# Four graph-attention layers in one kernel: nodes in strided chunks, attention vectors spread by TensorE, another order of the opening, a last step that ends chunk by chunk

## The chip, the core and the metric

The kernel runs on one NeuronCore of a Trainium2 chip, in one launch. The metric is device time in microseconds (us), from the first to the last instruction of the core. Before the change the time is 2699.22 us (median of 3 runs, 2696.39 to 2703.35).

The engines are named as in the profile: PE is TensorE's matmul, PEld its loading of the stationary operand, DVE is VectorE, ACT is ScalarE, POOL is GpSimd. SP only issues transfers. A "q" behind a name (SPq, ACTq) stands for the engine's own sequencer, where a DMA is issued. Each engine works through its instructions in the order in which the program gives them, so an instruction that waits holds up all that stand behind it on that engine.

## The reference

Sixteen graphs of 1024 nodes with 256 features go through four attention layers, all over the same adjacency matrix. Cut to what matters (`heads` is 4 with 64 features each in layers 0 and 2, and 1 with 256 features in layers 1 and 3):

```python
# x: (16, 1024, 256) float32, adj: (1024, 1024) int32 (about 3% ones)
for W, a in layers:
    h = maximum(layernorm(x), 0)
    q = (h @ W).reshape(B, N, heads, D)
    e = leaky_relu(q . a_src [:, i]  +  q . a_dst [:, j])    # for every pair i, j of nodes
    e = where(adj, e, -inf)
    x = x + act(softmax(e, axis=j) @ q)    # act: elu in layers 0 to 2, relu in layer 3
```

The 1024 x 1024 matrix of attention weights is made anew for each graph, layer and head: 16 x (4 + 1 + 4 + 1) = 160 times.

## The kernel before

A graph and a layer together are a **step**; there are 64 of them, numbered in the order in which the kernel takes them (four graphs, the streams, are in work at a time; the first six steps belong to the streams 0, 1, 2, 0, 3, 2). A step has a *preparation*, the *weights*, the *aggregation* and a *finish*. While one step is aggregated, the preparation of the next but one or so is put between the groups of its matmuls, by an agenda: the number of each piece says behind which group it comes.

Nodes lie on 128 partitions in 8 chunks. Before the change, node `c * 128 + p` is on partition `p` in chunk `c`, so that a graph's 1 MB comes in as pieces of 1 KB:

```python
def load(b, parts=1):
    xs[b] = xpool.tile([P, C, F], F32, name="x")          # P = 128, C = 8, F = 256
    xb = x[b].rearrange("(c p) f -> p c f", p=P)
    for i in range(parts):
        q = slice(i * C // parts, (i + 1) * C // parts)
        nc.sync.dma_start(out=xs[b][:, q], in_=xb[:, q])
```

The attention vectors of a layer are put on all partitions by the DMA itself, and two dot products with each row of W give the columns that are appended to W (on DVE):

```python
def vectors(queue=nc.sync):
    st["a"] = prep.tile([P, HALF, H, D], F32, name="e")
    for part in range(2):
        queue.dma_start(out=st["a"][:, part],
            in_=bass.AP(tensor=avs[l].tensor, offset=avs[l].offset + part * D,
                        ap=[[0, P], [hs, H], [1, D]]))      # step 0: the same row, 128 times
def columns():          # 4 products and 4 sums on DVE, and the squares for bound()
    ...
def bound():            # a matmul with ones, then DVE and POOL: biases for the exponentials
    ...
```

The adjacency is read once, in 8 blocks of 128 rows. For each block DVE takes the sign as bf16, PE turns it, DVE makes the 0/1 mask of layers 0 and 1 and ACT that of layers 2 and 3:

```python
def fetch_rows():  nc.sync.dma_start(out=st["raw"], in_=adj[c * P:(c + 1) * P, :])
def sign():        nc.vector.tensor_scalar(st["sgn"][:, 0], st["raw"], -1.0, 1.0, op0=max, op1=min)
def turn():        # 8 transposes of 128 x 128; four PSUM buffers hold the results
    for jc in range(C):
        nc.tensor.transpose(pm[:, jc, :], st["sgn"][:, 0, jc * P:(jc + 1) * P], identb)
def positive():    nc.vector.tensor_scalar(masks[0][:, :, c * P:(c + 1) * P], st["pm"], 0.0, None, is_gt)
def nonzero():     nc.scalar.activation(masks[1][:, :, c * P:(c + 1) * P], st["pm"], AF.Square)
```

The preparation of a step is a list of 20 pieces: `stats(0)`, `stats(1)` (DVE: `bn_stats` of four chunks each, then the reciprocal deviations), `normalise(0)`, `normalise(1)` (ACT), for each half two `transpose` (PE, evacuated by ACT with a relu) and four `project` (PE: four matmul instructions per chunk of nodes; ACT and POOL evacuate), then `factors` (ACT: exponentials), `rows` (PE turns the row factors, ACT copies them, SP writes them to DRAM), `fetch_heads` (SP reads them back, spread over all partitions: `gs`), and an empty one.

The weights of a head are 8 tiles of 128 x 1024, made from the spread row factors `g` (copied to PSUM by ACT), the column factors and the mask:

```python
def weights(n, h, jc):                                     # 18 buffers
    w = work.tile([P, N], F32, name="w", bufs=WBUFS)
    nc.vector.scalar_tensor_tensor(w, st["g", h], st["rcol"][:, jc, h:h + 1], mask[:, jc, :],
                                   op0=ALU.max, op1=ALU.mult)

def aggregate(n, h, i0, per):      # a group: four chunks of a head, or one where heads = 1
    ...                            # PE: sums over jc of w.T @ [q, 1]
    nc.scalar.activation(st["y"][:, i0:i0 + per, h, :], acc, AF.Copy)
```

`finish` works on all 8 chunks of the step: DVE takes the reciprocals, POOL scales in two halves, DVE adds to x in two halves, SP stores in two halves:

```python
def divide():      nc.vector.reciprocal(st["r"], st["y"][:, :, :, D])
def scaled(half):  nc.gpsimd.tensor_tensor(yh, yh, r..., op=mult)
def add(half):     nc.vector.scalar_tensor_tensor(xh, yh, 0.0, xh, op0=max, op1=add)   # last layer
def store(half):   nc.sync.dma_start(out=out[b, half * HALF * P:...].rearrange("(c p) f -> p c f", p=P), in_=...)
```

The opening, up to the main loop:

```python
load(0, 2)                                   # x of graph 0 in two halves, SP
layer[0][0](nc.scalar)                       # vectors of layer 0, on ACT's queue
load_weights(0, nc.scalar)                   # W of layer 0, on ACT's queue
for c in range(C): blocks[c][0]()            # adjacency, SP
load(1); load_weights(1)
...
first[0](); first[1](); first[2]()           # step 0: stats, stats, normalise
layer[0][1]()                                # columns
first[3](); ...                              # normalise; sign, turn, bound, transpose, project
...                                          # and the masks, in turns
for _ in range(2): agenda.pop(0)[2]()        # stats of step 1
emit_tiles(C, must=True)                     # weights of step 0, head 0
prepare(-1)                                  # the rest of the preparation of step 1
for i in range(2, STREAMS):
    load_weights(i); load(i)                 # x of graphs 2 and 3
# main loop: groups of step 0, ...
```

The agenda of step 1 is `[-2] * 10 + [-1] * 10`: all of its preparation stands ahead of the first group of step 0. The pieces `vectors`, `columns` and `bound` of the layers 1, 2 and 3 come behind the groups 0, 1 and 7 counted from step 0 group 1, step 3 group 3 and step 5 group 3.

Of the kernel before, what the change touches and what calls it, by code (L numbers as in the profile page):

```python
# [20 lines left out]
F32 = mybir.dt.float32  # L24
# [18 lines left out]
AFTER_FOUR = (-3, -2, -1, 0, 1, 1, 2, 2, 3, 3, 4, 4, 5, 5, 6, 6, 7, 8, 8, 10)  # L43
SOON = (0, 0, 1, 2, 3, 3, 4, 4, 5, 5, 5, 5, 6, 6, 7, 7, 8, 9, 9, 11)
AFTER_ONE = (0, 1, 2, 3, 4, 4, 5, 5, 6, 6, 7, 7, 8, 8, 9, 9, 10, 11, 11, 13)
LATE = (0, 0, 1, 1, 2, 2, 3, 3, 3, 3, 3, 3, 4, 4, 4, 4, 5, 6, 6, 8)


# [9 lines left out]
def kernel(ctx: ExitStack, tc: tile.TileContext, x, adj, ws, avs, out):  # L58
# [47 lines left out]
    def weight_columns(l):  # L106

        H, slope, hs, _ = LAYERS[l]
        D = F // H
        st = {}  # L110

        def vectors(queue=nc.sync):
            st["a"] = prep.tile([P, HALF, H, D], F32, name="e")
            for part in range(2):
                queue.dma_start(
                    out=st["a"][:, part],
                    in_=bass.AP(tensor=avs[l].tensor, offset=avs[l].offset + part * D,
                                ap=[[0, P], [hs, H], [1, D]]),
                )

        def columns():
            for k in range(K):
                for part in range(2):
                    prod = st["a"][:, 2 + part]
                    nc.vector.tensor_mul(
                        prod, wx[l][:, k, 0:F].rearrange("p (h d) -> p h d", h=H),
                        st["a"][:, part])
                    nc.vector.tensor_reduce(
                        wx[l][:, k, F + part * H:F + (part + 1) * H], prod, AX.X, ALU.add)
            st["sq"] = small.tile([P, K, H], F32, name="sq", bufs=1)  # L130
            wd = wx[l][:, :, F + H:F + 2 * H]
            nc.vector.tensor_tensor(st["sq"], wd, wd, op=ALU.mult)

        def bound():

            pn = ps_p.tile([P, H], F32, name="pp")
            for k in range(K):
                nc.tensor.matmul(pn, lhsT=ones, rhs=st["sq"][:, k, :], start=(k == 0),
                                 stop=(k == K - 1))
            top = small.tile([P, 1], F32, name="top", bufs=1)  # L140
            nc.vector.tensor_reduce(top, pn, AX.X, ALU.max)
            nc.gpsimd.tensor_tensor(top, top, half1, op=ALU.pow)
            nc.gpsimd.tensor_scalar(cbias[l], top, 16.01, None, op0=ALU.mult)
            nc.gpsimd.tensor_scalar(nbias[l], top, -16.01 * slope, None, op0=ALU.mult)
            nc.gpsimd.tensor_scalar(rbias[l], top, -16.01 * (1.0 - slope), SHIFT,
                                    op0=ALU.mult, op1=ALU.add)

        return vectors, columns, bound

    pairs = {}  # L150

    def mask_rows(c):

        st = {}

        def fetch_rows():
            st["raw"] = work.tile([P, N], I32, name="w", bufs=WBUFS)
            nc.sync.dma_start(out=st["raw"], in_=adj[c * P:(c + 1) * P, :])

        def sign():  # L160
            st["sgn"] = work.tile([P, 2, N], BF16, name="w", bufs=WBUFS)
            nc.vector.tensor_scalar(st["sgn"][:, 0], st["raw"], -1.0, 1.0, op0=ALU.max,
                                    op1=ALU.min)

        def turn():

            if c < HALF:
                if c % 2 == 0:
                    pairs[c // 2] = ps_g.tile([P, 2, C, P], BF16, name="g")
                pm = pairs[c // 2][:, c % 2]  # L170
            else:
                pm = ps_acc.tile([P, C, P], BF16, name="acc")
            st["pm"] = pm
            for jc in range(C):
                nc.tensor.transpose(pm[:, jc, :], st["sgn"][:, 0, jc * P:(jc + 1) * P], identb)

        def positive():
            nc.vector.tensor_scalar(masks[0][:, :, c * P:(c + 1) * P], st["pm"], 0.0, None,
                                    op0=ALU.is_gt)

        def nonzero():
            nc.scalar.activation(masks[1][:, :, c * P:(c + 1) * P], st["pm"], AF.Square)

        return fetch_rows, sign, turn, positive, nonzero

    def load(b, parts=1):
        xs[b] = xpool.tile([P, C, F], F32, name="x")
        xb = x[b].rearrange("(c p) f -> p c f", p=P)
        for i in range(parts):
            q = slice(i * C // parts, (i + 1) * C // parts)  # L190
            nc.sync.dma_start(out=xs[b][:, q], in_=xb[:, q])

    def preparation(n):
# [6 lines left out]
        def stats(half):  # L200
            if half == 0:
                st["bn"] = small.tile([P, C, 6], F32, name="bn")
            bn = st["bn"]
            for c in range(half * HALF, (half + 1) * HALF):
                nc.vector.bn_stats(bn[:, c, :], xs[b][:, c, :])  # L205
            if n == 0:
                combine(slice(half * HALF, (half + 1) * HALF), nc.vector)
            elif half == 1:
                combine(slice(0, C), nc.gpsimd)

        def combine(q, engine):

# [12 lines left out]
            engine.tensor_tensor(rstd, rstd, dev, op=ALU.add)  # L225
            nc.gpsimd.tensor_tensor(rstd, rstd, neghalf[:, q], op=ALU.pow)  # L226
            engine.tensor_tensor(shift, m0, m1, op=ALU.add)  # L227
            engine.tensor_tensor(shift, shift, rstd, op=ALU.mult)
            engine.tensor_scalar(shift, shift, -0.5, None, op0=ALU.mult)  # L229

# [84 lines left out]
    def aggregate(n, h, i0, per):  # L315
# [7 lines left out]
        for q in range(per):  # L323
            for jc in range(C):

                for o in range((i0 + q) * P, (i0 + q + 1) * P, cols):
                    nc.tensor.matmul(acc[o % P:o % P + cols, q, :],  # L327
                                     lhsT=st["w", h, jc][:, o:o + cols],
                                     rhs=st["whx"][:, jc, h, :], start=(jc == 0),
                                     stop=(jc == C - 1))  # L330
        nc.scalar.activation(st["y"][:, i0:i0 + per, h, :], acc, AF.Copy)  # L331

    def finish(n):
# [37 lines left out]

        def store(half):
            nc.sync.dma_start(
                out=out[b, half * HALF * P:(half + 1) * HALF * P, :].rearrange(
                    "(c p) f -> p c f", p=P), in_=xs[b][:, half * HALF:(half + 1) * HALF, :])
            if half == 1 and b + STREAMS < B:
                load(b + STREAMS)

# [61 lines left out]
    for n, (b, l) in enumerate(steps):  # L440
# [9 lines left out]
        if free > start + kind[0]:  # L450
            kind = LATE
            start = max(free, agenda_of[-1][0] + 5)
        agenda_of.append([start + k for k in kind] if n > 1 else [-2] * 10 + [-1] * 10)
        if n > 2:

            was = agenda_of[n - 1]
# [3 lines left out]
    with tc.manual_schedule():  # L460
        blocks = [mask_rows(c) for c in range(C)]
        layer = [weight_columns(l) for l in range(L)]
        load(0, 2)
        layer[0][0](nc.scalar)
        load_weights(0, nc.scalar)
        for c in range(C):
            blocks[c][0]()
        load(1)
        load_weights(1)
        nc.scalar.activation(warm, half1, AF.Exp)  # L470
        nc.vector.tensor_copy(identb, ident)
        first = [piece for _, piece in preparation(0)]

        turned, signed, masked = iter(range(C)), iter(range(C)), iter((0, 4, 5, 6, 1, 2, 3, 7))

        def sign_and_mask(second=True):
            c = next(signed, None)
            if c is not None:
                blocks[c][1]()
                blocks[c][2]()  # L480
            if second:
                c = next(turned, None)
                if c is not None:
                    blocks[c][3]()

        def other_mask(count):
            for _ in range(count):
                c = next(masked, None)
                if c is not None:
                    blocks[c][4]()  # L490

        first[0]()
        first[1]()
        first[2]()
        layer[0][1]()
        first[3]()
        sign_and_mask(False)
        layer[0][2]()
        sign_and_mask()
        for at in (4, 10):  # L500
            first[at]()
            first[at + 1]()
            sign_and_mask()
            first[at + 2]()
            first[at + 3]()
            sign_and_mask()
            other_mask(1)
            first[at + 4]()
            first[at + 5]()
            sign_and_mask()  # L510
            other_mask(1)
        for piece in first[16:]:
            piece()
        sign_and_mask()
        other_mask(C)
        done["prepared"] = 1
        plan(1)
        planned = 2
        for _ in range(2):
            agenda.pop(0)[2]()  # L520
        emit_tiles(C, must=True)
        prepare(-1)
        for i in range(2, STREAMS):
            load_weights(i)
            load(i)

        for l, at in ((1, 1), (2, 8 * 3 + 3), (3, 8 * 5 + 3)):
            for i, piece in zip((0, 1, 7), layer[l]):
                later[at + i] = piece
        for n in range(len(steps)):  # L530
            for k, (h, i0, per) in enumerate(groups(n)):
# [13 lines left out]
                emit_tiles(min(done["tiles"] + ahead, done["free"] + WBUFS))  # L545
            for _, piece in ending:
                piece()
            ending = finish(n)
        for _, piece in ending:
            piece()  # L550


def order_of_steps(B, L):
# [30 lines left out]
```

## Time and profile before

| | |
|---|---|
| span of the profiled execution | 2700.4 us |
| PE busy | 2567.4 us, 95% of the span |
| PEld busy | 2271.1 us, 84% |
| DVE busy | 1903.4 us, 70% |
| ACT busy | 1228.1 us, 45% |
| POOL busy | 987.8 us, 37% |
| DMA: mean rate, share of the main queue | 48 GB/s, 13.7% |
| mean granted clock of TensorE | 0.984 of full speed |
| transfers of x: 15 of 1024 KB, 2 of 512 KB | in pieces of 1 KB |

The page of the profile gives busy times and a strip of 40 slices. Where an engine that is busy nearly all the time stands still is seen better in tables of chosen stretches (busy time of each engine in each) and in the timeline. In the timeline a row has the start, the time taken from the first to the last instruction of the row, the engine, the line of the kernel, the operation, what it writes and reads with shapes, and how many instructions are merged in the row. The bracket at its end says how long the engine had been idle and what released it.

### The profile page before, as it was taken

The numbers are of one execution on the slowest core, as the hardware profiler recorded it, in microseconds if no ns is written. First come the engines' busy times: TensorE is split into PE (matmuls) and PEld (weight loads), VectorE is DVE, ScalarE is ACT, GpSimd is POOL, SyncE is SP. The second block draws the span as 40 slices with busy tenths as digits, with TensorE's granted clock in tenths as the row PEclk, the third lists the DMA queues.
The fourth block names the chain that finished last, engine by engine and source line by source line (L and its number), as shares of the span: only waits on it lengthen the run. The fifth ranks groups of instructions, "written<-read, shape, count | busy, mean of one in ns | idle before, by whom it ended". The sixth has DMA issues, their size and how long they took to land.

```text
span 2700.4 us, 89532 instructions
## 1 busy us (share of the span) xinstructions
PE 2567.4 (95%) x40080; PEld 2271.1 (84%) x40080; DVE 1903.4 (70%) x2059; ACT 1228.1 (45%) x3338; POOL 987.8 (37%) x1234
## 2 busy tenths in 40 slices
PE   4899999999999999999999999999999999999998
PEld 3787888888888888888888888888888888788876
DVE  5796586477785688667875778748687567678742
ACT  4343445445444544554444554544435444444431
POOL 2143433532514434344242353452342443443321
PEclk8899999999999999999999999999999999999999
DMA  4211101112012111002211201101202110111011
GB/s 137 76 42 37 30 26 41 35 62 81 26 61 67 42 42 33 18 33 72 73 34 49 72 33 43 41 25 57 80 27 72 63 41 19 34 40 43 33 33 55
DMA packets 63694, 130.12 MB, mean 48 GB/s; under 512 B 6224, under 2 KB 41808, under 8 KB 63312
## 3 DMA queue, kind: packets, MB, share of 16 engines
q1 hardware_dynamic: 61984, 123.88, 13.7%
q8 instruction: 316, 5.18, 0.8%
q10 hardware_dynamic: 1328, 0.52, 0.1%
q14 instruction: 66, 0.54, 0.1%
HBM read 106.95 MB, written 17.43 MB: 46 GB/s over the span
## 4 chain that ended last, share of the span: by engine, by line
PE 82%; DVE 8%; ACT 4%; issue 3%; POOL 2%; DMA 1%; DVEq 0%; SPq 0%; ACTq 0%; POOLq 0%
PE acc L327 61%; PE pp L255 17%; DVE w L311 6%; PE pp L243 4%; DVE bn L205 1%; ACT xn L235 1%; DMA wx<-in_L_gnn_W 1%; POOL rstd L226 1%; ACT whx L257 1%; ACT g L306 0%; ACT e L361 0%; ACT whx L261 0%; PE pp L282 0%; ACT y L331 0%; POOL y L352 0%
## 5 line engine op out<-in xcount | busy, mean ns | idle before, releaser
L327 PE MATMUL acc<-whx,w 128*64 128x65 f32 x36864 | 1951.8, 242 | 41.3 <-DVE w L311 30.4
L327 PEld LDWEIGHTS acc<-whx,w 128*64 128x64 f32 x36864 | 1768.0, 146 | 223.5 <-issue 69.9
L311 DVE SCALAR_TENSOR_TENSOR w<-g,rcol,mask 128x1024 f32<-128x1024 f32 x1280 | 1544.1, 1274 | 440.5 <-ACT g L306 394.6
L331 ACT ACTIVATE y<-acc 128x260 f32<-128x260 f32 (+1 forms) x512 | 196.5, 384 | 1089.8 <-PE acc L327 1089.7
L255 PE MATMUL pp<-wx,hT 128*128 128x258 f32 (+1 forms) x2048 | 514.1, 394 | 5.7 <-ACT hT L244 3.2
L352 POOL TENSOR_TENSOR y<-y,r 128x1024 f32<-128x1024 f32 x128 | 242.3, 1897 | 618.0 <-DVE r L348 614.4
L255 PEld LDWEIGHTS pp<-wx,hT 128*128 128x128 f32 x2048 | 376.2, 191 | 75.1 <-ACT whx L261 6.0
L266 POOL TENSOR_TENSOR whx<-whx 128x256 f32<-128x256 f32 x256 | 160.0, 629 | 461.5 <-ACT whx L264 460.4
L368 POOL TENSOR_TENSOR x<-x,e 128x1024 f32<-128x1024 f32 x96 | 226.6, 2365 | 274.7 <-DVE e L367 250.1
L235 ACT ACTIVATE xn<-x,shift,rstd 128x256 f32<-128x256 f32 x512 | 264.2, 590 | 135.0 <-POOL shift L229 122.4
L367 DVE SCALAR_TENSOR_TENSOR e<-e,y 128x1024 f32<-128x1024 f32 x96 | 117.7, 1226 | 197.1 <-ACT e L361 197.1
L257 ACT ACTIVATE whx<-pp,nbias 128x4 f32<-128x4 f32 (+1 forms) x512 | 134.9, 264 | 166.4 <-PE pp L255 155.2
L243 PE MATMUL pp<-ident,xn 128*128 128x128 f32 x1024 | 158.7, 288 | 43.7 <-ACT xn L235 34.1
L205 DVE BATCH_NORM_STATS2 bn<-x 128x6 f32<-128x256 f32 x512 | 173.0, 407 | 28.5 <-DMA x<-in_x 25.8
L243 PEld LDWEIGHTS pp<-ident,xn 128*128 128x128 f32 x1024 | 117.1, 144 | 82.5 <-ACT xn L235 43.8
L306 ACT ACTIVATE g<-gs 128x1024 f32<-128x1024 f32 x160 | 162.4, 1018 | 8.4 <-DVE w L311 5.4
L244 ACT ACTIVATE hT<-pp 128x512 f32<-128x512 f32 x256 | 142.9, 592 | 26.6 <-PE pp L243 24.5
L261 ACT ACTIVATE whx<-pp,whx 128x256 f32<-128x256 f32 x256 | 121.4, 474 | 0.0
L220 POOL TENSOR_TENSOR dev<-bn 128x8 f32<-128x8 f32 x63 | 16.1, 256 | 276.5 <-DVE bn L205 276.5
L361 ACT ACTIVATE e<-e 128x1024 f32<-128x1024 f32 x96 | 100.8, 1050 | 30.0 <-POOL e L357 30.0
L226 POOL TENSOR_TENSOR rstd<-rstd,neghalf 128x8 f32<-128x8 f32 (+1 forms) x65 | 107.0, 1646 | 19.2 <-DVE shift L227 14.3
L357 POOL TENSOR_SCALAR e<-y 128x1024 f32<-128x1024 f32 x96 | 99.8, 1040 | 8.4
(58 smaller groups left out, 550.7 us busy)
## 6 DMA issues: line engine op xcount, KB each, us to landing
gs<-grow SPq DMA_DIRECT2D x160, 512.0 KB
out<-x SPq DMA_DIRECT2D x32, 512.0 KB
x<-in_x SPq DMA_DIRECT2D x15, 1024.0 KB
w<-in_adj SPq DMA_DIRECT2D x8, 512.0 KB
x<-in_x SPq DMA_DIRECT2D x2, 512.0 KB
wx<-in_L_gnn_W SPq DMA_DIRECT2D x3, 256.0 KB
e<-in_L_gnn_a SPq DMA_DIRECT2D x6, 128.0 KB
grow<-gT SPq DMA_DIRECT2D x32, 16.0 KB
```

The lines of the kernel that those rows point to most:

```text
L205: nc.vector.bn_stats(bn[:, c, :], xs[b][:, c, :])
L235: nc.scalar.activation(xn[:, q, :], xs[b][:, c, :], AF.Identity, bias=st["shift"][:, c:c + 1], scale=st["rstd"][:, c:c + 1])
L243: nc.tensor.transpose(pt[:, q, :], st["xn", half][:, q, k * P:(k + 1) * P], ident)
L255: nc.tensor.matmul(pw, lhsT=st["hT", half][:, k, q * P:(q + 1) * P], rhs=wx[l][:, k, :], start=(k == 0), stop=(k == K - 1))
L257: nc.scalar.activation(whx[:, c, :, D], pw[:, F + H:F + 2 * H], AF.Exp, bias=nbias[l], scale=slope)
L266: nc.gpsimd.tensor_tensor(whx[:, c, :, 0:D], whx[:, c, :, 0:D], whx[:, c, :, D:D + 1].to_broadcast([P, H, D]), op=ALU.mult)
L306: nc.scalar.activation(g, state[n]["gs", h], AF.Copy)
L311: nc.vector.scalar_tensor_tensor(w, state[n]["g", h], state[n]["rcol"][:, jc, h:h + 1], masks[LAYERS[steps[n][1]][3]][:, jc, :], op0=ALU.m ...
L327: nc.tensor.matmul(acc[o % P:o % P + cols, q, :], lhsT=st["w", h, jc][:, o:o + cols], rhs=st["whx"][:, jc, h, :], start=(jc == 0), stop=(j ...
L331: nc.scalar.activation(st["y"][:, i0:i0 + per, h, :], acc, AF.Copy)
L352: nc.gpsimd.tensor_tensor(yh, yh, r[:, :, None].to_broadcast([P, HALF * H, D]), op=ALU.mult)
L368: nc.gpsimd.tensor_add(xh, xh, e)
```

## The change

The change has four parts.

**Nodes in strided chunks.** Node `p * 8 + c` is now on partition `p` in chunk `c`. A partition's share of a graph is one run of 8 KB in DRAM (4 KB where half a graph is moved). The rows of the adjacency are fetched to match, and the transposes of the mask read every eighth column.

**Attention vectors broadcast by TensorE.** The DMA brings the two vectors to one partition only. A new piece, `spread`, multiplies a row of ones with them (PE, 512 columns into PSUM) and ACT copies the result to SBUF. For the layers 1 to 3 it comes one group behind `vectors`, and `columns` and `bound` move by one group.

**The opening in another order.** The vectors of layer 0 are issued first, W of layer 0 goes behind x on SP's queue and ahead of the adjacency, and the combining of the statistics is cut in two. The mask work is ordered block by block. The agenda of step 1 becomes `FIRST`: its transposes and projections are put between the groups 0 to 3 of step 0, and the loads of x for graphs 2 and 3 are so issued ahead of step 1's row factors.

**The last step ended by chunks.** In the last step each chunk is divided, passed through the relu, added and stored as soon as its matmuls are done.

```diff
+FIRST = (-2, -2, -1, -1, 0, 0, 0, 0, 1, 1, 1, 1, 2, 2, 2, 2, 3, 3, 3, 5)
 ...
         def vectors(queue=nc.sync):
             st["a"] = prep.tile([P, HALF, H, D], F32, name="e")
-            for part in range(2):
-                queue.dma_start(out=st["a"][:, part], in_=bass.AP(..., ap=[[0, P], [hs, H], [1, D]]))
+            queue.dma_start(out=st["a"][0:1, 2:4], in_=bass.AP(..., ap=[[0, 1], [D, 2], [hs, H], [1, D]]))
+
+        def spread():
+            pa = ps_p.tile([P, 2, H, D], F32, name="pp")
+            nc.tensor.matmul(pa..., lhsT=ones[0:1, :], rhs=st["a"][0:1, 2:4]..., start=True, stop=True)
+            nc.scalar.activation(st["a"][:, 0:2], pa, AF.Copy)
 ...
-            nc.sync.dma_start(out=st["raw"], in_=adj[c * P:(c + 1) * P, :])
+            nc.sync.dma_start(out=st["raw"], in_=adj.rearrange("(p c) j -> p c j", p=P)[:, c])
 ...
+            sgn = st["sgn"][:, 0].rearrange("p (q c) -> p c q", c=C)
             for jc in range(C):
-                nc.tensor.transpose(pm[:, jc, :], st["sgn"][:, 0, jc * P:(jc + 1) * P], identb)
+                nc.tensor.transpose(pm[:, jc, :], sgn[:, jc, :], identb)
 ...
-        xb = x[b].rearrange("(c p) f -> p c f", p=P)
+        xb = x[b].rearrange("(p c) f -> p c f", p=P)          # the stores likewise
 ...
             if n == 0:          # stats: combine is cut in two
+                if half == 1: combine_end(first half)
                 combine(q, nc.vector)
+                if half == 1: combine_end(second half)
 ...
+        if n == len(steps) - 1:                                # in aggregate, the last step
+            nc.vector.reciprocal(r, acc[:, 0, D:D + 1])
+            nc.vector.tensor_scalar(y, acc[:, 0, 0:D], r, 0.0, op0=ALU.mult, op1=ALU.max)
+            nc.vector.tensor_add(xs[b][:, i0, :], xs[b][:, i0, :], y)
+            nc.sync.dma_start(out=out[b]...[:, i0], in_=xs[b][:, i0, :])
+            return
 ...                             # opening
+        layer[0][0](nc.scalar)
         load(0, 2)
-        layer[0][0](nc.scalar)
-        load_weights(0, nc.scalar)
+        load_weights(0)
 ...                             # adjacency, load(1), load_weights(1)
+        layer[0][1]()                                          # spread
+        for i in (0, 1, 2, 3): first[i]()                      # stats, stats, normalise, normalise
+        layer[0][2]()                                          # columns
+        first[4](); first[5]()                                 # transposes of half 0
+        layer[0][3]()                                          # bound
+        sign(0)                                                # sign and turn of block 0
+        for i, c in ((6, 1), (8, 2), (10, 3), (12, 4), (14, 5)):
+            first[i](); first[i + 1]()                         # two projections, or two transposes
+            sign(c)                        # sign and turn of block c, mask of block c - 1 (DVE)
+        for piece in first[16:]: piece()                       # factors, rows, fetch_heads
+        for c in (4, 5, 0, 1, 2, 3): blocks[c][4]()            # masks on ACT
+        sign(6); sign(7); sign(8)
 ...                             # stats of step 1, weights of head 0
+        blocks[6][4](); blocks[7][4]()
         prepare(-1)
         for i in range(2, STREAMS): load_weights(i); load(i)
-            for i, piece in zip((0, 1, 7), layer[l]):
+            for i, piece in zip((0, 1, 2, 8), layer[l]):
-            ending = finish(n)
+            ending = finish(n) if n < len(steps) - 1 else []
```

## The prediction, written before the result

> **What bounds the kernel now.** I read the page's busy times first, then its strip, then a table of stretches, then the timeline of the two ends.
>
> ```profile
> PE 2567.4 (95%) x40080; PEld 2271.1 (84%) x40080; DVE 1903.4 (70%) x2059; ACT 1228.1 (45%) x3338; POOL 987.8 (37%) x1234
> ...
> PE   4899999999999999999999999999999999999998
> ```
>
> TensorE is the bound: 2567.4 us of matmuls in a span of 2700.4. The change takes no matmul away, so at most the 133 us in which PE stands still can be won. The strip puts a good part into its first slice of 67.5 us (digit 4) and a little into the last (8). A table of four stretches sharpens that; its columns are the stretch, its length, then busy time (and count) of each engine, the granted clock, the DMA share and GB/s:
>
> ```profile
> 0.00:103.00 103.00, 51.78 (x676) 42.78 (x678) 56.79 (x99) 41.74 (x105) 21.52 (x52) 0.85 0.37 124
> 103.00:135.00 32.00, 30.38 (x699) 27.09 (x695) 32.00 (x28) 11.97 (x37) 4.91 (x8) 1.00 0.15 52
> 135.00:2689.00 2554.00, 2485.02 (x38714) 2201.24 (x38713) 1810.37 (x1931) 1174.03 (x3196) 957.60 (x1172) 0.99 0.14 45
> 2689.00:2701.00 12.00, 0.20 (x1) 0.00 (x0) 4.24 (x3) 0.38 (x1) 3.74 (x2) 0.68 0.25 87
> ```
>
> PE idles 51 us before 103 us, 69 us spread over the 2554 us of the middle, and 12 us at the end. Three parts of the change aim at the 51 and the 12; only the longer pieces of x reach the middle.
>
> The opening in the timeline, the rows where the path turns:
>
> ```profile
> 22.14 0.43 DVE L125 TENSOR_TENSOR e<-wx,e 128x256 f32<-128x256 f32 x1 [3.93 <-DMA wx<-in_L_gnn_W]
> ...
> 32.67 2.83 PE L255 MATMUL pp<-wx,hT 128*128 128x264 f32 x8
> ...
> 53.66 1.03 ACT L306 ACTIVATE g<-gs 128x1024 f32<-128x1024 f32 x1 [2.61 <-DMA gs<-grow]
> 54.73 9.63 DVE L311 SCALAR_TENSOR_TENSOR w<-g,rcol,mask 128x1024 f32<-128x1024 f32 x8 [5.93 <-ACT g L306]
> ...
> 73.70 7.69 PE L327 MATMUL acc<-whx,w 128*64 128x65 f32 x256
> 74.10 0.66 SPq L286 DMA_DIRECT2D grow<-gT  x1
> 75.31 0.46 SPq L191 DMA_DIRECT2D x<-in_x  x1
> 81.66 2.71 DVE L205 BATCH_NORM_STATS2 bn<-x 128x6 f32<-128x256 f32 x8 [17.30 <-DMA x<-in_x]
> ...
> 93.95 9.28 PE L327 MATMUL acc<-whx,w 128*64 128x65 f32 x228 [0.71 <-DVE w L311]
> ```
>
> Three things hold the opening up. W of layer 0 lands at 22.1 and everything on DVE behind it waits. The first weights start only at 54.73. And from 64.4 to 81.7 DVE waits 17.3 us for x of graph 2, whose transfer stands on SP behind step 1's row factors (74.10); PE runs out of weights at 81.4 and is fed one tile at a time until 93.95. Step 0's last group (the eighth run of 128 aggregation matmuls) starts at 124.94 and ends at 128.9. That is the time to compare.
>
> The end:
>
> ```profile
> 2689.24 0.38 ACT L331 ACTIVATE y<-acc 128x257 f32<-128x257 f32 x1 [3.10 <-PE acc L327]
> ...
> 2690.00 3.74 POOL L352 TENSOR_TENSOR y<-y,r 128x1024 f32<-128x1024 f32 x2 [21.98 <-DVE r L348]
> 2691.93 4.03 DVE L370 SCALAR_TENSOR_TENSOR x<-y,x 128x1024 f32<-128x1024 f32 x2 [2.07 <-POOL y L352]
> ```
>
> After the last matmul (2689.2) come ACT, two POOL halves, two DVE halves until 2696.0, and the store of the second half, issued at 2696.0: 11.2 us to the end.
>
> **What the Trainium skill says.** "DMA: Bandwidth & Descriptors", section "Queues, rings and completion order", says that the queues of SP and ACT share the same 16 engines, each of which takes turns between them. The trace agrees that ACT's queue is no fast lane: W was issued on it at 1.85 and landed at 22.05, while SP's queue carried x and the adjacency. "TensorE: Matmul & The Clock Gate", section "Part 1: The HAM clock gate", says that TensorE drops to half its clock after an idle window of about 3.4 us and needs as much activity to come back. The trace agrees: granted clock 0.50 from 93 to 97 us, 0.63 to 100, 1.00 after. "SBUF — State Buffer", section "Door 1: The DMA port swizzle", says that SBUF has lines of 16 bytes and that an access crossing to a new line pays. The new transposes step 8 bf16, exactly 16 bytes; no run here shows what that costs.
>
> **Part by part.**
>
> *Opening, until the first projection (before 32.67).* In the first 10 us the DMA moved 97 GB/s, in pieces of 256 B and 1 KB; from 20 to 30 us, with many 4 KB rows, 348 GB/s. x and W are 1.31 MB, at 348 GB/s 3.8 us. With 0.7 us to the issue and 1.9 us of latency (the small row-factor write took 1.87) the halves of x land at about 4.5 and 6, W at about 7. DVE then runs without a gap: statistics of half 0 (1.4 + 1.1), of half 1 (1.4), combining with the power on POOL in it (2.9), from 4.5 to 11.3. The columns took 3.45 us from 22.14: to 14.8. Bound matmul, maximum and first sign 1.5 us, first turn 1.0 us: the first projection at about **18**, 14.7 us earlier.
>
> *From there to the first weights.* Before, 32.67 to 54.73: 22.1 us. It holds the same 8 projections, transposes and turns, PE-bound, then factors, row factors, write, read back and `g`. One ACT mask (1.04 us) leaves the path. The six masks on ACT now stand in the DMA wait before `g`: 6 x 1.03 = 6.2 us against 47.46 to 53.66, also 6.2, so they just fit. I add 1 to 2 us for the strided turns. First weights at **40.5** instead of 54.7.
>
> *Step 0.* Now step 1's transposes and projections are between the groups. From the first weights: eight tiles at 1.206 us gate group 0, 9.65. The rest of group 0, 100 matmuls at the slow 40.7 ns (9.28 us for 228), 4.1. Seven groups at 3.93: 27.5. Step 1: transposes 1.9 + 1.45 (first pair cold), eight projections at 1.03 with some cold, 8.5, rows 0.3. Step 2: transposes 1.1 + 1.45, six projections 6.15. `spread` of layer 1: 512 columns; a projection's four instructions take 1.0 us for twice 264 columns, so 1.0. Sum 63.1: step 0 ends at **103.6** instead of 128.9, **−25**. DVE needs 32 tiles (38.6), statistics of step 2 (2.7) and columns (3.4), 44.7, so it would be done by 85 and PE sets the end. The 17.3 us wait disappears, since x of graphs 2 and 3 is issued around 38 us.
>
> *The end.* Per chunk: reciprocal 0.2, scaling from PSUM 0.4, addition 0.4 (L125, the same size, took 0.416), issue and landing 3.4 (before: 4.4 from 2696.0 to the end for four times the bytes). Total 4.5 instead of 11.2: **−6.7**. The other seven chunks end beside matmuls of 3.5 us each.
>
> *`spread` for layers 2 and 3* adds 1.0 us of PE each on the path. For layer 3 the vectors were issued at 328.46, after SP had waited for a buffer that POOL frees, and DVE began at 331.8. The new matmul stands behind the next group, which ended at about 330.2, so PE may wait 1 us. **+3**.
>
> *x in 8 KB pieces.* 15 loads and 32 stores become shorter, but nobody waits for them later: behind 100 us ACT waits 0.2 us in all for a spread row, and all waits of DVE for x (25.8 us) lie in the opening. **0**.
>
> Sum: −25 − 6.7 + 3 = −29 from 2699: **2670**.
>
> **Rivals.**
> *DVE becomes the bound of step 0.* For it: from 101.9 to 135.4 it makes 28 tiles without a gap. Against: 44.7 us of work in a stretch of 63, though the 18 buffers make it stop in between. If it binds, a tile or two late at several groups, about +5: 2675.
> *The strided turns become the wait.* 40 of them (five blocks) lie between the first projection and the row factors. If each takes 0.1 to 0.3 us more, 4 to 12 us come back: 2674 to 2682. Against: DVE's sign and mask (1.85 us a block) hide part.
> *The DMA stays the brake.* The rows of a block are now 32 KB apart in DRAM. Were they slow, masks and x of graph 1 would come late and the 40.5 would be 46 or more: 2676.
> *Shorter transfers help the middle.* Then the 69 us of idle PE there would shrink and the time could fall to 2650. Against: the waits above; PE's longest there are for ACT's normalising (24.8 us) and for weights (21.2), neither held by a transfer.
> *The groups of the middle fall otherwise.* An agenda that begins 25 us earlier may fit a little better or worse: 5 us either way.
>
> **Range and chances.** The rivals that cost (5, 8, 6) are not additive and each has perhaps one chance in four; the gain in the middle has one in ten. Hence 2669 as the centre, and 2656 to 2684 for 8 in 10. Two per cent is 54 us, below 2645; even the whole 51 us of the opening and 7 at the end would hardly reach it, and the opening can't lose all its idle time. So within 2% has 0.95, faster 0.04, slower 0.01.
>
> **What would show it.** DVE's first column product at about 11 us with W long landed; first projection near 18; first weights near 40; no wait of DVE for x at step 2; end of step 0 near 104; PE's idle time until step 0 ends down from 52 us (of 128.9) to some 29 (of 104); 4 to 5 us from the last matmul to the end; and the middle, from the end of step 0 to the end of the last matmul, 2560 us before (128.9 to 2689.2), longer by about the 3 us of `spread`. The prediction is wrong if the first weights come after 46 us, if PE waits for weights throughout step 0, or if the middle moves by more than 10 us.

## The result and the profile after

The changed kernel takes 2669.98 us (median of 4 runs, 2666.09 to 2673.08) against 2699.3 us before; the ratio is 0.989, 95% interval 0.9871 to 0.9909. The forecast was 2669. It is a gain of 29 us, and as the forecast had it, it is made in the first 104 us and the last 11 us.

The page after, busy times and strip:

```profile
PE 2568.9 (96%) x40088; PEld 2268.3 (85%) x40088; DVE 1906.4 (71%) x2080; ACT 1229.8 (46%) x3334; POOL 983.2 (37%) x1232
...
PE   6999999999999999999999999999999999999999
```

PE does the same work (2568.9 us of it), and the first digit of the strip has gone from 4 to 6, the last from 8 to 9. The table of stretches, cut this time at the first weights, at the end of step 0 and behind the last matmul (columns as before: stretch, length, busy time and count of PE, PEld, DVE, ACT, POOL, granted clock, DMA share, GB/s):

```profile
0.00:41.06 41.06, 21.49 (x119) 15.50 (x119) 25.75 (x62) 21.95 (x52) 9.87 (x24) 0.91 0.52 196
41.06:104.10 63.04, 54.71 (x1116) 47.25 (x1116) 52.16 (x57) 30.43 (x84) 15.61 (x34) 0.89 0.27 92
104.10:2663.00 2558.90, 2492.74 (x38858) 2205.54 (x38854) 1827.47 (x1962) 1177.39 (x3199) 957.74 (x1174) 0.99 0.14 45
2663.00:2667.00 4.00, 0.00 (x0) 0.00 (x0) 0.97 (x3) 0.00 (x0) 0.00 (x0) 0.82 0.09 33
```

The four lengths before were 54.7, 74.2, 2560.3 and 11.2 us. So 13.7 us come from the stretch up to the first weights, 11.1 from step 0, 7.2 from the end and 1.6 from the middle, where nothing was expected to shrink. (These are two profiled executions, 2700.4 and 2666.9 us; their difference is 33, that of the medians 29.) PE's idle time until the end of step 0 fell from 52.8 us of 128.9 to 27.9 of 104.1, where some 29 had been forecast.

The opening in the timeline after:

```profile
11.40 0.42 DVE L134 TENSOR_TENSOR e<-wx,e 128x256 f32<-128x256 f32 x1
...
17.70 3.26 PE L274 MATMUL pp<-wx,hT 128*128 128x264 f32 x8
...
34.31 1.22 DVE L188 TENSOR_SCALAR mask<-acc 128x1024 uint8<-128x1024 bf16 x1 [2.90 <-ACT mask L192]
...
38.44 2.70 DVE L215 BATCH_NORM_STATS2 bn<-x 128x6 f32<-128x256 f32 x8
38.49 1.03 ACT L325 ACTIVATE g<-gs 128x1024 f32<-128x1024 f32 x1 [0.59 <-DMA gs<-grow]
...
41.06 9.61 DVE L330 SCALAR_TENSOR_TENSOR w<-g,rcol,mask 128x1024 f32<-128x1024 f32 x8
...
41.63 0.46 SPq L201 DMA_DIRECT2D x<-in_x  x1
...
50.58 2.70 DVE L215 BATCH_NORM_STATS2 bn<-x 128x6 f32<-128x256 f32 x8
```

The first column product (22.14 before) waits for nothing any more. `g` is ready at 39.5, and the weights at 41.06 come straight after the statistics of step 1: it is DVE itself that sets their start. DVE was that late because its mask work had stood still for 2.90 us (the row at 34.31), until ACT had made the first two of its own masks. The statistics of step 2 (50.58) have no bracket at all; before, 17.30 us of waiting for x stood there. The last group of step 0 starts at 100.22 and ends at 104.2.

The end:

```profile
2662.89 0.17 DVE L355 RECIPROCAL rlast<-acc 128x1 f32<-128x1 f32 x1 [2.33 <-PE acc L346]
2663.10 0.48 DVE L356 TENSOR_SCALAR y<-acc,rlast 128x256 f32<-128x256 f32 x1
2663.62 0.43 DVE L357 TENSOR_TENSOR x<-x,y 128x256 f32<-128x256 f32 x1
```

Three short DVE instructions and one store of 128 KB are all that follows the last matmul: 4.0 us.

### The profile page after: what moved, and what is told of

Its sections match the earlier page's. It is cut to its first block, busy times and chain, and to the rows that moved or that the text cites. A ratio compares the mean times of both kernels' runs of the same rounds, so it can differ in the third digit from the quotient of the medians.

```text
span 2666.9 us, 89560 instructions
## 1 busy us (share of the span) xinstructions
PE 2568.9 (96%) x40088; PEld 2268.3 (85%) x40088; DVE 1906.4 (71%) x2080; ACT 1229.8 (46%) x3334; POOL 983.2 (37%) x1232
## 4 chain that ended last, share of the span: by engine, by line
PE 83%; DVE 8%; ACT 4%; issue 3%; POOL 2%; DMA 0%; DVEq 0%; ACTq 0%
PE acc L346 62%; PE pp L274 17%; DVE w L330 6%; PE pp L262 4%; DVE bn L215 1%; ACT xn L254 1%; POOL rstd L242 1%; ACT g L325 1%; ACT whx L276 1%; ACT e L391 0%; ACT whx L280 0%; PE pp L301 0%; ACT y L361 0%; ACT whx L283 0%; DVE e L397 0%
```

## The experiments

The places in time come from one profile of each run. "First weights" is the start of the first tile of weights, "step 0" the end of its last group, "middle" from there to the end of the last matmul, "end" what follows. Each ratio is to executions of the kernel before that were measured beside the run (medians of 2699.3 to 2701.5 us).

| run | median us | ratio to before (95%) | first weights | step 0 | middle | end |
|---|---|---|---|---|---|---|
| before | 2699.3 | | 54.7 | 128.9 | 2560.3 | 11.2 |
| changed | 2670.0 | 0.989 (0.9871 to 0.9909) | 41.1 | 104.2 | 2558.7 | 4.0 |
| changed, again | 2671.2 | 0.9893 (0.988 to 0.9906) | 40.7 | 103.7 | 2560.8 | 4.1 |
| e1 old end | 2676.2 | 0.9912 (0.9895 to 0.993) | 42.0 | 105.6 | 2558.4 | 10.4 |
| e2 old agenda | 2681.4 | 0.993 (0.9917 to 0.9942) | 40.8 | 117.4 | 2557.9 | 4.4 |
| e3 old agenda, loads first | 2669.0 | 0.9878 (0.9863 to 0.9893) | 41.8 | 104.6 | 2552.7 | 4.5 |
| e4 pieces of 1 KB | 2666.6 | 0.9874 (0.986 to 0.9887) | 40.4 | 103.6 | 2557.3 | 3.8 |
| e5 W on ACT's queue | 2671.0 | 0.9894 (0.9878 to 0.9909) | 41.4 | 104.6 | 2564.3 | 4.2 |
| e6 vectors by DMA | 2678.3 | 0.9921 (0.9908 to 0.9934) | 48.3 | 110.3 | 2561.6 | 4.6 |
| e7 spread eleven times | 2693.0 | 0.9975 (0.9964 to 0.9985) | 41.9 | 105.3 | 2585.2 | 4.0 |
| e8 half of step 1 early | 2665.1 | 0.987 (0.9854 to 0.9885) | 41.0 | 102.3 | 2559.5 | 4.0 |
| b1 before, loads first | 2681.9 | 0.9935 (0.9922 to 0.9948) | 55.1 | 114.4 | 2555.6 | 11.2 |
| b2 before, spread | 2688.8 | 0.9961 (0.9948 to 0.9974) | 44.2 | 118.2 | 2557.5 | 11.1 |
| f1 half early, 1 KB | 2666.4 | 0.9875 (0.9862 to 0.9888) | 39.9 | 100.0 | 2560.5 | 3.9 |

Leaving e7 out, the middle lies between 2552.7 and 2564.3 us in versions that hardly differ in it. So a difference of a few us in the whole time is not to be read as an effect; the places in the opening are steadier: the first weights come between 40.7 and 42.0 us in the executions that have the changed kernel's code up to there.

### The end alone

```diff
-        if n == len(steps) - 1:          # the chunked ending in aggregate
+        if False:
...
-            ending = finish(n) if n < len(steps) - 1 else []
+            ending = finish(n)
+        for _, piece in ending: piece()
```

> The changed kernel, with the old ending of the last step (all chunks to SBUF, then reciprocals, two halves on POOL and DVE, two stores of 512 KB). Theory (the parts add up): the stretch behind the last matmul grows from 4.1 us to about 11.2 as before the change, nothing else moves: 7 us slower than the changed kernel, 2677 us, 0.992 of the kernel before. Rival (the short DVE instructions and eight stores of the chunked ending hold the last groups back a little, so that part of its gain is lost again): the matmuls of the last step get shorter gaps here, and the time is at most 4 us above the changed kernel, 2674 or less.

Measured: 2676.2 us, 5 to 6 above the two measurements of the changed kernel, and 10.4 us behind the last matmul instead of 4.0. The theory's 7 is slightly large. The medians do not exclude that a little is lost again in the last groups, but the last matmuls show the same row in both profiles: 114 in 25.05 and 25.06 us. So the chunked ending costs PE nothing in these 25 us, and the part is worth about 6 us.

### What step 0 won: the place of the loads, not of the matmuls

```diff
-FIRST = (-2, -2, -1, -1, 0, 0, 0, 0, 1, 1, 1, 1, 2, 2, 2, 2, 3, 3, 3, 5)
+FIRST = [-2] * 10 + [-1] * 10
```

> The changed kernel with the old agenda for step 1: all of its preparation ahead of the first group of step 0, and so the loads of x for graphs 2 and 3 on SP behind its row factors. Theory: DVE waits again some 15 to 17 us for x of graph 2, the first weights stay at 41 us, step 0 ends 11 us later than 104.1, at about 115; 2681 us, 0.993 of before. Rival (what the new order of the opening won was the earlier start alone, and PE, which can now prepare step 1 while the first weights are made, catches up): step 0 ends at 106 or earlier, 2672 us.

The second run has this edit and one more:

```diff
-        prepare(-1)
         for i in range(2, STREAMS):
             load_weights(i); load(i)
+        prepare(-1)
```

> As the run with the old agenda, but with the loads of W and x for graphs 2 and 3 issued ahead of step 1's preparation. Theory (the wait of DVE for x of graph 2 was the loss, not where step 1's matmuls stand): DVE does not wait for x, step 0 ends at 104 to 107, time 2670 to 2673. Rival (putting the matmuls between the groups is itself worth most of the 11 us): step 0 ends at 112 or later, 2678 or more, hardly better than the old agenda alone.

What DVE waited for in the first 120 us (in total, times, longest), first with the old agenda, then with the loads moved ahead of it:

```profile
DVE bn L215 <- DMA x<-in_x: 23.4, 2, 20.4
```

```profile
DVE bn L215 <- DMA x<-in_x: 3.1, 1, 3.1
```

With the old agenda the wait for x of graph 2 is back, at 20.4 us, step 0 ends at 117.4 and the time is 2681.4. With the loads first it is gone, step 0 ends at 104.6 and the time is 2669.0, the changed kernel's. Both came out close to what the theory had, with the wait some 3 us longer than its 15 to 17 and the end of step 0 2 us later than its 115. Where step 1's matmuls stand makes no difference to step 0: it took 63 us from the first weights either way (63.1 in the changed kernel, 62.8 in e3).

The same single move in the kernel **before**:

> The kernel before, with one move only: W and x of graphs 2 and 3 are issued ahead of step 1's preparation, so that they no longer stand on SP behind its row factors. Theory (this wait alone cost the 11 us that step 0 lost): first weights at 54.7 as before, DVE does not wait for x of graph 2, step 0 ends at 116 to 118 instead of 128.9, 2687 to 2689 us, 0.9955 of before. Rival (the new agenda or the earlier start is needed for it): step 0 ends at 124 or later, 2694 or more.

In its timeline x is issued at 57.20, right behind step 0's row factors and ahead of step 1's (which come at 74.32):

```profile
57.20 0.46 SPq L191 DMA_DIRECT2D x<-in_x  x1
...
66.85 2.71 DVE L205 BATCH_NORM_STATS2 bn<-x 128x6 f32<-128x256 f32 x8 [2.12 <-DMA x<-in_x]
...
73.93 15.15 PE L327 MATMUL acc<-whx,w 128*64 128x65 f32 x512
```

The wait falls from 17.30 to 2.12 us, and PE goes through four groups (512 matmuls) without a gap where it had run dry after two. Step 0 ends at 114.4, 14.5 us earlier; 2681.9 us, 17 below before. That is more than expected, and the largest single part of the gain. It is a swap of two statements.

With the loads in the same order, step 0 takes 59.3 us from the first weights in b1 and 62.8 in e3. The first matmuls of step 1, in b1 and then in e3, show where most of the difference lies:

```profile
56.90 2.81 PE L243 MATMUL pp<-ident,xn 128*128 128x128 f32 x8 [9.12 <-ACT xn L235]
```

```profile
46.83 2.80 PE L262 MATMUL pp<-ident,xn 128*128 128x128 f32 x8 [8.84 <-ACT xn L254]
```

They start 1.8 us after the first weights (55.11) in b1 and 5.0 us after them (41.79) in e3. In b1 the statistics of step 1 had ended at 49.4, while DVE still waited for `g`; with the new opening they end only as the first weights begin, and what POOL and ACT make of them comes after that. The `spread` of layer 1 takes another 1.1 us of PE. So the new opening gives back some 3.5 us of what the order of the loads wins.

### What the opening won: the small pieces of the broadcast

Four runs take apart the 13.7 us up to the first weights. Longer pieces of x, W's queue, the vectors and the order of the pieces had all been changed at once.

The old layout of the nodes, with x in 1 KB pieces in and out:

```diff
-        xb = x[b].rearrange("(p c) f -> p c f", p=P)       # and the stores, and the rows of adj
+        xb = x[b].rearrange("(c p) f -> p c f", p=P)
-            sgn = st["sgn"][:, 0].rearrange("p (q c) -> p c q", c=C)
+            sgn = st["sgn"][:, 0].rearrange("p (c q) -> p c q", c=C)
```

> The changed kernel with the old layout of the nodes: x in pieces of 1 KB in and out, adjacency rows of a block next to each other, transposes of the mask without a stride. Everything else as changed. Theory (no one waits for a transfer of x in the middle, and x in short pieces comes only a little later once W and the vectors don't compete): first bn_stats at 5.5 to 6 instead of 4.9, first weights 1 to 2 us later, middle unchanged within 4 us, 2671 to 2673 us. Rival A (the short pieces were what made x and W late in the opening): second half of x at 10 us or later, first weights at 45 or later, 2674 or more. Rival B (8 KB pieces pay in the middle): the middle, 2559 us, grows by more than 8, 2680 or more.

W on ACT's queue again:

```diff
-        load_weights(0)
+        load_weights(0, nc.scalar)
```

> The changed kernel with W of layer 0 issued on ACT's queue again, behind the small attention vectors, not on SP's ahead of the adjacency. Theory A (W came late because the 1024 small pieces of the broadcast vectors stood ahead of it on the same queue; they are gone): W lands by 9 us, columns still at 11.4, first weights at 41, 2670 us. Theory B (it was the competition with x and the adjacency on SP's queue, as the prediction had it): W lands at 15 us or later, columns and first weights move by 4 us or more, 2674 or more.

The vectors put on all partitions by the DMA again, everything else as changed:

```diff
-            queue.dma_start(out=st["a"][0:1, 2:4], in_=... ap=[[0, 1], [D, 2], [hs, H], [1, D]])
+            for part in range(2):
+                queue.dma_start(out=st["a"][:, part], in_=... ap=[[0, P], [hs, H], [1, D]])
...          # and no spread()
```

> The changed kernel without the spreading matmuls: the vectors of all four layers are put on all partitions by the DMA, as before, those of layer 0 on ACT's queue; W of layer 0 stays on SP's. Theory A (the many small pieces hold up both queues): the halves of x land at 8 and 12 us or later although they come in 4 KB pieces, the vectors at about 18 to 20 us, the first column product near 19 and not 11.4, first weights at 48 to 50, time 2677 to 2679. Theory B (pieces of x and the place of W were what mattered): x at 5 and 7 as now, vectors by 12 us, first weights at 42 or earlier, 2671 or less.

And the kernel before with that part alone changed:

```diff
+            if l == 0:
+                queue.dma_start(out=st["a"][0:1, 2:4], ...); return
...
+        layer[0][3]()          # spread, ahead of step 0's preparation
```

> The kernel before, with one part only: the attention vectors of layer 0 come to one partition and are spread by a matmul; W stays on ACT's queue, x in 1 KB pieces, the order as before. Theory (the 1024 small pieces of the broadcast held up both queues): x at 5 and 7 us, W by 10, first column product at 12 to 13 instead of 22.1, first weights at 45 to 46, the wait for x of graph 2 stays, 2689 to 2691 us. Rival (the order of the opening was needed too): first weights at 50 or later, 2695 or more.

The first 10 us of five kernels, same columns as above. First the kernel before (1 KB pieces, vectors by DMA):

```profile
0.00:10.00 10.00, 0.00 (x0) 0.00 (x0) 2.00 (x8) 1.49 (x2) 0.95 (x10) 1.00 0.38 97
```

The changed kernel (4 KB pieces, vectors to one partition):

```profile
0.00:10.00 10.00, 2.26 (x3) 0.68 (x3) 4.98 (x25) 2.96 (x5) 1.98 (x11) 1.00 0.81 275
```

With 1 KB pieces (e4):

```profile
0.00:10.00 10.00, 2.33 (x3) 0.68 (x3) 5.01 (x25) 3.03 (x5) 2.01 (x12) 1.00 0.80 289
```

With 4 KB pieces, the vectors by DMA (e6):

```profile
0.00:10.00 10.00, 0.00 (x0) 0.00 (x0) 2.61 (x12) 1.49 (x2) 1.99 (x11) 1.00 0.25 76
```

The kernel before with the vectors to one partition (b2):

```profile
0.00:10.00 10.00, 2.04 (x2) 0.49 (x2) 4.19 (x18) 3.25 (x6) 1.98 (x11) 1.00 0.79 276
```

The last column is the answer: 275, 289, 276 GB/s without the broadcast, whatever the length of the pieces of x; 76 and 97 with it. The DMA share beside it, 0.25 in e6, says that the 16 engines were not busy with the small pieces either: they stood idle three quarters of the time. The rate is not low from the start: in e6 it is 242 GB/s from 2 to 4 us, which brings the first half of x, and then 37, 19 and 69 in the next three stretches of 2 us. DVE in e6:

```profile
5.01 1.41 DVE L224 BATCH_NORM_STATS2 bn<-x 128x6 f32<-128x256 f32 x4 [3.28 <-DMA x<-in_x]
...
12.30 1.41 DVE L224 BATCH_NORM_STATS2 bn<-x 128x6 f32<-128x256 f32 x4 [4.73 <-DMA x<-in_x]
...
18.84 0.42 DVE L143 TENSOR_TENSOR e<-wx,e 128x256 f32<-128x256 f32 x1 [2.45 <-DMA wx<-in_L_gnn_W]
```

The second half of x and W are on SP's queue and are still late, W until 18.8 although it stands ahead of the adjacency. So the broadcast, 1024 pieces of 256 B on ACT's queue, holds up both queues. First weights come at 48.3 (expected 48 to 50), and the time is 2678.3. Only the first half of x came sooner than this theory expected. e5 shows the other side: W on ACT's queue behind the *small* vectors costs nothing, with columns at 11.38 and 2671.0 us. And in b2 the one part brings the first weights from 54.7 to 44.2 and the time to 2688.8, 10.5 us below before. The other 3 us, down to 41.1, are left to the new order of the pieces in the opening; no run tries it alone.

With 1 KB pieces (e4) not one place in the opening is later (first statistics at 4.8 us, first projection at 17.6), where 1 to 2 us had been expected, and the time is 2666.6, a little below the changed kernel's. Of the strided layout only its small cost can be seen, in a turn of eight transposes at full clock. The changed kernel, then e4:

```profile
27.87 0.71 PE L185 MATMUL acc<-identb,w 128*128 128x128 bf16 x8
```

```profile
27.37 0.62 PE L185 MATMUL acc<-identb,w 128*128 128x128 bf16 x8
```

That is 0.09 us a block. Six such turns stand ahead of the row factors, so about half a us of the opening could be theirs, but the first weights can't show it: 40.4 in e4 lies only 0.3 us below the earliest of the executions with strided turns. The size of a turn agrees in kind with the page "SBUF — State Buffer" of the Trainium skill (section "Door 1: The DMA port swizzle"): crossing a 16-byte line at each element has a price, and here it is 15% of a turn. Why the whole time of e4 is 3 to 5 us lower is not settled; the middle of its profile is within the spread of the others.

### What a spreading matmul costs in the middle

```diff
+            for _ in range(11 if l > 1 else 1):
                 nc.tensor.matmul(pa..., lhsT=ones[0:1, :], rhs=st["a"][0:1, 2:4]..., start=True, stop=True)
```

> The changed kernel with the spreading matmul of layers 2 and 3 done eleven times into the same tile and not once: 20 more at 1.12 us of PE each. Theory (PE sets the pace of the middle, so its work adds in full, as the prediction had it for the two single ones): 22 us slower than the changed kernel, 2692. Rival (idle time of PE nearby takes it up, which is why the middle did not grow by 3 us): at most 15 us slower, 2685 or less.

It repeats work and computes the same. 2693.0 us, 22 to 23 above the changed kernel: the number of the theory by luck, since the cost of one matmul was not what it had. The row of eleven in layer 2, and the table of two stretches inside it:

```profile
218.74 14.76 PE L126 MATMUL pp<-e,ones 1*128 1x512 f32 x22
```

```profile
219.00:225.00 6.00, 6.00 (x13) 2.52 (x13) 4.95 (x5) 0.24 (x1) 0.00 (x0) 0.85 0.06 21
225.00:233.00 8.00, 8.00 (x10) 2.76 (x9) 0.00 (x0) 0.00 (x0) 0.00 (x0) 0.50 0.00 0
```

The profile shows PE busy for all of the 8 us, and its clock falls to 0.50. The two rows of eleven took 14.76 and 16.93 us, 31.7 together where two single ones take 2.24. Of the 29.4 us added, 22 to 23 reach the medians. A part of the rest is taken up by idle time of PE: it idles 62.2 us in the middle of this profile, against 66.0 and 68.7 in the two of the changed kernel. A wait of 4.38 us for ACT's normalising, which ends at 233.7 in the first of these, soon after the `spread` of layer 2, is gone in e7. So twice 1.1 us may well vanish in the same way, but the runs cannot tell 2 us from the spread of the middle (e6 has no spreading matmul at all and a middle of 2561.6).

### A step further

In the changed kernel PE gets four matmuls per tile of weights from 42 to 51 us. The statistics of step 1 now go ahead of the last mask pieces, and half of step 1's transposes and projections ahead of group 0:

```diff
-FIRST = (-2, -2, -1, -1, 0, 0, 0, 0, 1, 1, 1, 1, 2, 2, 2, 2, 3, 3, 3, 5)
+FIRST = (-2, -2, -1, 0, -1, -1, -1, -1, -1, -1, 1, 1, 2, 2, 2, 2, 3, 3, 3, 5)
...
-        sign(6); sign(7); sign(8)
         done["prepared"] = 1; plan(1); planned = 2
         for _ in range(2): agenda.pop(0)[2]()
+        sign(6); sign(7); sign(8)
         emit_tiles(C, must=True)
-        blocks[6][4](); blocks[7][4]()
         prepare(-1)
+        blocks[6][4](); blocks[7][4]()
```

> A further step from the changed kernel: the statistics of step 1 go ahead of the last three mask pieces on DVE, and the first half of step 1's transposes and projections ahead of group 0, into the 10 us in which PE gets only four matmuls per weight tile. Theory (the gated stretch has room for it): first weights at 39 to 40, step 0 ends at 98 to 99 instead of 104.1, 2664 to 2665 us. Rival (normalising and evacuation on ACT and the half clock of an idle PE make these pieces end later than the tiles): group 0 ends only at 58 or later, step 0 at 102 or later, 2668 or more.

It fell between the two. PE took step 1's pieces from 42.7 to 50.0 at a mean clock of 0.72, then waited 1.65 us for POOL and began group 0 at 51.6. Two groups then ran in one go, but step 0 ended at 102.3, only 2 us earlier, because the first weights did not come sooner:

```profile
40.96 9.63 DVE L330 SCALAR_TENSOR_TENSOR w<-g,rcol,mask 128x1024 f32<-128x1024 f32 x8 [1.15 <-ACT g L325]
```

DVE, which has done the statistics earlier here, waits 1.15 us for `g`. The median of 2665.1 us is the theory's number, but step 0 accounts for 2 us of the gain only. Where the rest comes from the profile can't show: its middle is no shorter (2559.5 us), and its execution was the slowest of the four (2667.6 us). With the layout of e4 added, and the changed kernel measured beside it:

> The run with half of step 1 prepared early, with the old layout of the nodes (1 KB pieces, transposes without a stride). Theory: both steps keep their small effects, step 0 ends at 101 to 102, 2663 to 2665 us. Rival: the differences of a few us between these versions are the spread of the runs, 2666 to 2670.

> The changed kernel once more, on the chip and in the rounds of the other runs of this call, to compare them with it. All theories: 2666 to 2673 us, step 0 ends at 103 to 105.

f1 ends step 0 at 100.0 (103.7) and takes 2666.4 us (2665.5 to 2667.8) against 2671.2 (2670.3 to 2672.8). It beats both kernels, the changed one by 4.8 us. Since e4 alone takes 2666.6, what each of the two edits adds to that stays open.

## Why the prediction was right, point by point

**Up to the first projection** (18 predicted, 17.70 measured) the size was right and the cause was not. The prediction counted x and W at the rate of a stretch with 4 KB rows, 348 GB/s, and explained the slow start by pieces of 256 B and of 1 KB and by ACT's queue being "no fast lane". The runs show that the length of x's pieces plays no part (e4) and that ACT's queue does not either (e5). It is the broadcast of the vectors alone that keeps both queues at 76 to 97 GB/s instead of 275 (e6, b2). That the number came out is luck in this sense: the change removed the real cause along with the supposed ones. The page "DMA: Bandwidth & Descriptors" of the Trainium skill (section "Queues, rings and completion order") lets the queues take turns. The trace of e6 shows more than turns: the shared engines stand idle while both queues are late.

**From there to the first weights** 22.5 us were predicted, 23.4 measured. The six masks on ACT fitted into `g`'s wait for the DMA, as counted: behind them ACT waited another 0.59 us for the spread row. But DVE stood still for 2.90 us until the first two of them were done, and so its last masks and its statistics of step 1 ended 1.5 us after `g` (ready at 39.5). The sum had only the path over `g` and not the one over the masks and the statistics on DVE.

**Step 0** was predicted at 63.1 us and took 63.1. The sum of PE's pieces was right because DVE stayed ahead and no load stood in the way; e2, e3 and b1 show that the wait for x was the whole of what had been lost there. Its terms came within 1.3 us each and not closer: PE waited 1.26 us for ACT's factors of step 1, which the sum did not have, and the first transposes took 1.1 us, not 1.9. The agreement to a tenth is luck. The new agenda mattered only for putting the loads ahead; the interleaving itself brought nothing to step 0.

**The end**: 6.7 us predicted, 7.2 in the profile, 6.4 in e1's. **The pieces of 8 KB**: 0 predicted and 0 found, in the middle as in the opening.

**The spreading matmuls** at +3 us are the term that was mis-sized. Each took its 1.12 us and PE did not wait for the vectors of layer 3; the middle is 1.6 us shorter in one profile of the changed kernel and 0.5 us longer in the other, not 3 longer. e7 puts the price of many of them at about three quarters of what PE spends, and leaves that of two below what can be seen.

**The rivals.** DVE did not bind step 0: once the first eight tiles were made, PE did not wait for weights again until it ended. The strided turns cost 0.09 us a block, not 0.8 to 2.4. The adjacency's distant rows were no brake: the DMA moved 405 GB/s from 10 to 20 us. The parts tried alone in the kernel before (10.5 us for the vectors, 17 for the loads) and the end (6) add up to 33 or 34, more than the 29 of the whole; the 3.5 us that step 0 lasts longer with the new opening than in b1 (59.3 against 62.8) are of that size.

## What to carry to other kernels

Before lengthening the pieces of a large transfer, look for a broadcast that runs beside it: one of 2 KB to 128 partitions in 256 B pieces cost 7 us here (e6) to 10 (b2), and a matmul of 2 us with a copy of 0.6 replaced it. A load whose buffer is free should not be issued behind one that waits for a computation on the same in-order queue; that order alone was worth 14.5 us at the end of step 0. Where one engine is the bound, count its work from a milestone in the trace to the next; sums of that kind came within 1 us here, while whole times of the changed kernel lay up to 7 us apart (2666.1 to 2673.1). A piece of work that fits into one engine's wait may still hold up another engine: follow both paths to the place where they meet.

## What was not expected of the hardware

TensorE's clock fell to half although the profile shows PE busy without a break: in the 22 matmul instructions with one row of 128 in use (e7, from 218.74) it was 1.00 until 222 us and 0.50 from 224, and it was still at 0.64 on average in the 4 us of full matmuls from 234 us. The row in layer 3 shows the same, 0.50 from 325 to 333 us. The page "TensorE: Matmul & The Clock Gate" of the Trainium skill (section "Part 1: The HAM clock gate") ties the clock to how busy PE has been; in this run, time that the profile counts as busy does not account for it alone. The profile models where a matmul ends, so short gaps inside the row are not excluded. That fewer active rows are the reason is a guess, since no run varied their number.

With a broadcast by DMA the 16 engines were 75% idle in the first 10 us, and still all transfers together, those of the other queue among them, went at 76 GB/s instead of 275 (e6 and the changed kernel). Whether the writing of 1024 small descriptors holds up both queues, or the reading of one DRAM row by all, was not tried.
